# Expert passes of a fused transformer kernel: the low-rank product in five parts, the gate's second product two slots later, the output sums two slots apart, and a new end

## The chip, the cores and the metric

The kernel runs on one core of one Trainium2 chip. The metric is the device time of one execution in microseconds; before the change it is 2830.43 us, the median of three runs (2828.27, 2830.43 and 2831.24). All data are 32-bit floats.

## The reference

Four layers follow one another over 8 items of 512 x 512: a stencil on a grid, a transformer block (attention with 16 heads and a feed-forward part), one expert feed-forward block per item, and a low-rank "safety" layer. The change touches what follows the expert blocks:

```python
def expert(x, e):                      # Wi[e]: 512x2048, Wo[e]: 2048x512
    h = gelu(x @ Wi[e] + bi[e])
    r = h @ Wo[e] + bo[e] + x
    return layernorm(r) * gamma[e] + beta[e]

def safety(y, score):                  # y: 8 x 512 x 512, after the expert
    U_o, V_o = gram_schmidt(U), gram_schmidt(V)        # 512 x 32 each
    basis = U_o @ V_o.T
    h1 = relu(y.mean(axis=1) @ gate_w1.T + gate_b1)    # 128 per item
    strength = sigmoid(h1 @ gate_w2.T + gate_b2) * sigmoid(score)
    feats = (y @ basis) @ basis.T[:, :32]              # 512 x 32 per item
    return y + strength * (feats @ resp_w.T + resp_b + safety_bias)
```

`(y @ basis) @ basis.T[:, :32]` is one product of `y` with a 512 x 32 matrix. The kernel makes that matrix once and keeps it in the tile `wl3`.

## The kernel before, in words

The function `mlp_stage` runs 16 passes of the same form, q = 0 to 15: passes 0 to 7 are the feed-forward part of the transformer block, passes 8 to 15 the expert of items 0 to 7. A pass is `run(q, hooks)`. It has 56 slots. In slots 0 to 27 (four groups g of 7 slots, the seven products of a Strassen-like scheme) TensorE computes `u = A x B` from the weights `wi` and the turned input `bt`, VectorE (DVE) combines the seven products into `act`, and ScalarE (ACT) applies the gelu. In slots 28 to 55 (seven products of four slots, the name `y_28` to `y_52` giving the first slot) TensorE multiplies `act` with `wo`, and DVE adds the products into `x`. A slot is four 128x128x256 products, eight records in the trace. The products `u`, `y` and, in the last pass, a few small ones share six PSUM buffers (tag `u`); everything else that TensorE writes in this stage shares two (tag `tr`).

Everything else of a pass is hung onto the slots: `at(hooks, s, f)` calls f just before the products of slot s are issued. Each engine executes its own instructions strictly in the order in which they were written (`pin` keeps it), so a hook's instruction that has to wait holds back whatever stands behind it on its engine. DMA issues of the SyncE queue (SP) are ordered by the framework. All small products go through the helper `mm` (line 1137 of the profile), all transposes through `tp` (L1140), additions on DVE through `add` (L1143) and on GpSimd (POOL) through `gadd` (L1146).

The hooks that matter here:

- Passes 0 to 7 do the Gram-Schmidt steps of U and V (`gs_b`, the last of the 32 at slot 53 of pass 7). At slot 1 of pass 8 `low_rank` makes `wl3` from the result `qm`: it normalises `qm` (`square`, L1163; `inverse_norm`, a power on POOL at L1168; a scaling at L1201), turns it (`qtr`, copied to `qd`), and makes three small products, `pg`, `ph` and `pw`, each of which takes the DVE copy of the one before (`gram`, `hmat`). `wl3` is first read at slot 38 of pass 9.
- Passes 9 to 15 carry the tail of the item before, o = q - 1: `tail_norm` (slot 8, layer norm), `tail_turn` (slots 29 to 35, `ytr`, then `yT` on ACT, which also sums over the rows into `pool`), `tail_gamma` (37, DVE, L1569), `tail_feats` (38, product `pf`, copied to `ft`), `gate` (39, product `pg`, then two DVE instructions at L1617 and L1618 that make `h1`), `strength` (40, product `pz`, sigmoid on ACT, L1625), `add_beta` (42, DVE, then 128x2048 on POOL) and `tail_out` (50 to 53, one product `po` each, then on DVE at L1649 `x += st * po`; after each second one the rows go to DRAM).
- The same passes prepare the next one: `turn` (41, 43, 45, 47: `btr`), `w_quads` on POOL (46 and 50), `b_quads` on DVE (50: eight additions of 128x256, tiles `tb` and `bt`), and at slot 2 of the next pass `add_row`, 128x2048 on POOL.
- In pass 15 the first half of its own tail runs at slots 49 to 55 on rows 0 and 1. What follows the last slot works on rows 2 and 3: norm, turn, `pf`, gamma, beta, `gate` over the sum of both halves of `pool`, `strength`, and four times `tail_out`, where `po` is here the sum of two products (`rw` and `rb`).

Of the kernel before, what the change touches and what calls it, by code (L numbers as in the profile page):

```python
# [11 lines left out]
F32 = mybir.dt.float32  # L12
# [4 lines left out]
ALU = mybir.AluOpType  # L17
# [3 lines left out]
NB = 8  # L21
S = 512
D = 512
P = 128
R = 4
# [4 lines left out]
KC = D // P  # L30
RK = 32
# [1077 lines left out]
def mlp_stage(tc, a, small, xp, io, wo8, x1d, ident, eidx, sigs, layernorm, rstd_of, phalf, wl3, g2, b1, first):  # L1109
# [15 lines left out]
    nc = tc.nc  # L1125
# [3 lines left out]
    with ExitStack() as ctx:  # L1129
# [6 lines left out]
        def mm(out, lhsT, rhs, start, stop):  # L1136
            pin(nc.tensor.matmul(out, lhsT=lhsT, rhs=rhs, start=start, stop=stop))  # L1137

        def tp(out, src, idn=ident):
            pin(nc.tensor.transpose(out, src, idn))  # L1140

        def add(out, x, y, op=ALU.add):
            pin(nc.vector.tensor_tensor(out, x, y, op))  # L1143

        def gadd(out, x, y, op=ALU.add):
            pin(nc.gpsimd.tensor_tensor(out, x, y, op))  # L1146
# [13 lines left out]
        def square(src, other, tag):  # L1160
            junk = ap.tile([n, D], F32, name=f"junk_{tag}", tag="tmp", bufs=4)
            s = small.tile([n, 1], F32, name=f"{tag}_s", tag=f"{tag}_s")
            pin(nc.vector.tensor_tensor_reduce(junk, src, other, 1.0, 0.0, ALU.mult, ALU.add, s))  # L1163
            return s

        def inverse_norm(n2):
            d = small.tile([n, 1], F32, name="gs_d", tag="gs_d")
            pin(nc.gpsimd.tensor_tensor(d, n2, phalf[:n], ALU.pow))  # L1168
            pin(nc.vector.tensor_scalar(d, d, GS_EPS, None, ALU.add))
            r = small.tile([n, 1], F32, name="gs_r", tag="gs_r")  # L1170
            pin(nc.vector.reciprocal(r, d))
            return r
# [22 lines left out]
            if i + 1 < RK:  # L1195
                gs_a(i + 1)

        def low_rank():

            r = inverse_norm(square(qm, qm, "gn"))  # L1200
            pin(nc.vector.tensor_scalar(qm, qm, r, None, ALU.mult))  # L1201
            tr = ps.tile([P, KC, n], F32, name="qtr", tag="tr")
            for c in range(KC):
                tp(tr[:, c, :], qm[:, c * P : (c + 1) * P], ident[:n, :n])
            qd = ap.tile([P, KC, n], F32, name="qd", tag="beta", bufs=2)
            pin(nc.vector.tensor_copy(qd, tr))
            pg = ps.tile([RK, RK], F32, name="pg", tag="tr")
            for c in range(KC):
                mm(pg, qd[:, c, RK:n], qd[:, c, RK:n], c == 0, c == KC - 1)
            g = small.tile([RK, RK], F32, name="gram", tag="gram", bufs=1)  # L1210
            pin(nc.vector.tensor_copy(g, pg))
            ph = ps.tile([RK, RK], F32, name="ph", tag="tr")
            mm(ph, g, qm[0:RK, 0:RK], True, True)
            h = small.tile([RK, RK], F32, name="hmat", tag="hmat", bufs=1)
            pin(nc.vector.tensor_copy(h, ph))
            pw = ps.tile([P, KC, RK], F32, name="pw", tag="tr")
            for c in range(KC):
                mm(pw[:, c, :], qm[0:RK, c * P : (c + 1) * P], h, True, True)
            pin(nc.vector.tensor_copy(wl3, pw))


        b2 = ap.tile([P, D], F32, name="b2row", tag="bo_e", bufs=1)
# [333 lines left out]
        def tail_norm(q, rows):  # L1556

            if q not in outs:
                outs[q] = dict(
                    ft=ap.tile([P, P], F32, name=f"ft_{q}", tag="ft"), pooled=[],  # L1560
                )
            v = [xs[q][:, r, :] for r in rows]
            layernorm(v, v, LN_EPS2, "ln2", pin)
# [32 lines left out]
        def tail_feats(q, rows):  # L1596
            ys = outs[q]["ys"]
            pf = ps.tile([P, P], F32, name=f"pf_{q}_{rows[0]}", tag="tr")
            for c in range(KC):
                for i, r in enumerate(rows):  # L1600
                    mm(
                        pf[r * RK : (r + 1) * RK, :], wl3[:, c, :], ys[c][:, i, :],
                        c == 0, c == KC - 1,
                    )
            m = slice(rows[0] * RK, (rows[-1] + 1) * RK)
            pin(nc.vector.tensor_copy(outs[q]["ft"][m, :], pf[m, :]))
# [22 lines left out]
        def add_beta(q):  # L1629
# [2 lines left out]
            pin(nc.vector.scalar_tensor_tensor(beta, rb, st, beta, ALU.mult, ALU.add))  # L1632
            gadd(x, x, beta[:, None, :].to_broadcast([P, R, D]))

        def tail_out(q, rows):
            t = outs[q]
            x, ft, st = xs[q], t["ft"], t["st"]
            last = q == NQ - 1
            for r in rows:
                po = ps.tile(  # L1640
                    [P, D], F32, name=f"po_{q}_{r}", tag="u" if last else "tr",
                    bufs=6 if last else 2,
                )
                m = slice(r * RK, (r + 1) * RK)
                mm(po, ft[m, :], rw[m, :], True, not last)
                if last:
                    mm(po, ones[m, :], rb[m, :], False, True)
                pin(
                    nc.vector.scalar_tensor_tensor(x[:, r, :], po, st, x[:, r, :], ALU.mult, ALU.add)  # L1649
                )  # L1650
                if r % 2:
                    nc.sync.dma_start(
                        a["out"][q - NB].rearrange("(p r) f -> p r f", r=R)[:, r - 1 : r + 1, :],
                        x[:, r - 1 : r + 1, :],
                    )


        def at(hooks, s, f, *args):
            hooks.setdefault(s, []).append(lambda: f(*args))
# [8 lines left out]
        for q in range(NQ):  # L1668
            hooks = {}
            nx = q + 1 if q + 1 < NQ else None  # L1670

            at(hooks, 0, load_wo, q)
            if nx:
                if nx >= NB:
                    at(hooks, 45, load_extra, nx)
                at(hooks, 2, load_x, nx)
                for g in range(NG):
                    at(hooks, 7 * (g + 1), load_wi, nx, g)
            if 1 <= q <= NB:
                at(hooks, 4, lambda q=q: nc.sync.dma_start(x2d[q - 1], xs[q - 1]))  # L1680

            at(hooks, 2 if q else 26, add_row, q)
            at(hooks, 7, w_quads, q, 2, gadd)
            at(hooks, 14, w_quads, q, 3, gadd)
            for g in range(NG):
                at(hooks, 18 + 2 * g, t13, q, g)
            if nx:
                if nx < NB:
                    at(hooks, 33, norm, nx)
                for c in range(KC):  # L1690
                    at(hooks, 41 + 2 * c, turn, nx, c)
                at(hooks, 50, b_quads, nx)
                at(hooks, 46, w_quads, nx, 0, gadd)
                at(hooks, 50, w_quads, nx, 1, gadd)
            if q < NB:
                for i, s in enumerate((4, 18, 30, 53) if q else (18, 24, 30, 53)):
                    at(hooks, s, gs_b, 4 * q + i)
            if q == 0:
                at(hooks, 8, gs_a, 0)
                at(hooks, 10, load_constants)  # L1700
                at(hooks, 38, constants)
            if q == NB:
                at(hooks, 1, low_rank)
            elif q > NB:
                every = range(R)
                o = q - 1
                at(hooks, 8, tail_norm, o, every)
                for c in range(KC):
                    at(hooks, 29 + 2 * c, tail_turn, o, every, [c])
                at(hooks, 37, tail_gamma, o, every)  # L1710
                at(hooks, 38, tail_feats, o, every)
                at(hooks, 39, gate, o)
                at(hooks, 40, strength, o)
                at(hooks, 42, add_beta, o)
                for r in range(R):
                    at(hooks, 50 + r, tail_out, o, [r])
            if q == NQ - 1:
                half = range(0, 2)
                at(hooks, 49, tail_norm, q, half)
                for c in range(KC):  # L1720
                    at(hooks, 51 + c, tail_turn, q, half, [c])
                at(hooks, 55, tail_feats, q, half)
                at(hooks, 55, tail_gamma, q, half)
            run(q, hooks)
        q, half = NQ - 1, range(2, 4)
        x, beta = xs[q], extra[q][1][2]
        gadd(x[:, 0:2, :], x[:, 0:2, :], beta[:, None, :].to_broadcast([P, 2, D]))
        tail_norm(q, half)
        tail_turn(q, half, range(KC))
        tail_feats(q, half)  # L1730
        tail_gamma(q, half)
        add(x[:, 2:4, :], x[:, 2:4, :], beta[:, None, :].to_broadcast([P, 2, D]))
        gate(q)
        strength(q)
        tail_out(q, range(R))


# [86 lines left out]
```

## Time and profile before

The profile is of one execution of 2828.87 us; its span (first to last instruction) is 2826.4 us.

| what | value |
|---|---|
| median of three runs | 2830.43 us |
| profiled execution, its span | 2828.87 us, 2826.4 us |
| busy share of PE, DVE, ACT, POOL | 97%, 69%, 35%, 53% |
| mean granted TensorE clock | 0.989 |
| pass 7 (the last of the feed-forward part) | 98.45 us |
| pass 8 | 110.58 us |
| passes 9 to 14, each | 108.8 us |
| pass 15, slots 0 to 55 | 108.55 us |
| from the last product of slot 55 to the end of the span | 25.37 us |

PE is TensorE, PEld its weight loads, SPq the issue of DMAs. A pass is counted from the start of its first product `u` to that of the next pass, so its length says how far the pass is from the bare 98.45 us of the products. In lines of the timeline the first number is the start, the second the time from the first start to the last end of the group; `x8` is the number of records; a bracket names how long the engine sat idle before it and what ended the wait.

### The profile page before, as it was taken

The page shows a single profiled execution, that of the slowest core. Times are in us where ns is not written, and L with a number is a line of the kernel's source. Part 1 is how long each engine was busy: PE and PEld are TensorE (multiplying, and loading weights), DVE is VectorE, ACT ScalarE, POOL GpSimd, SP SyncE. Part 2 cuts the span into 40 slices and gives each one's busy share as a digit, 9 for nine tenths or more (in the row PEclk, how much of TensorE's full clock was granted, in tenths as well). Part 3 has the DMA queues.
Part 4 walks back from the last instruction along what each step waited for, and adds up shares of the span by engine and source line. Part 5 has one row for each costly group of instructions (what it writes and reads, how often), then busy time and mean ns, then how long its engine had stood idle before and what let it go on. Part 6 is the DMA issues. An engine that isn't in the chain of part 4 may idle for free.

```text
span 2826.4 us, 39775 instructions
## 1 busy us (share of the span) xinstructions
PE 2731.6 (97%) x14646; PEld 2013.2 (71%) x14646; DVE 1942.6 (69%) x3583; ACT 1003.3 (35%) x2133; POOL 1502.6 (53%) x1080
## 2 busy tenths in 40 slices
PE   5999999999999998999999999999999999999997
PEld 3455555555555554888888888887888888888885
DVE  6889898888888766576756666655466565556654
ACT  1466666666666666211211211111121121121120
POOL 3455555555555553566555656564455455445532
PEclk9999999999999999999999999999999999999998
DMA  9665757666665554642444253343224233133110
GB/s 303 220 211 173 235 176 239 203 210 215 190 228 187 162 156 144 190 125 71 120 140 123 51 157 123 80 122 123 98 68 138 78 105 124 63 131 112 45 71 30
DMA packets 190399, 405.60 MB, mean 144 GB/s; under 512 B 24104, under 2 KB 28784, under 8 KB 183934
## 3 DMA queue, kind: packets, MB, share of 16 engines
q1 hardware_dynamic: 185192, 391.93, 41.8%
q0 software_dynamic: 3680, 11.07, 3.1%
q8 instruction: 116, 1.90, 0.3%
q14 instruction: 77, 0.63, 0.1%
q10 hardware_dynamic: 1334, 0.07, 0.0%
HBM read 367.32 MB, written 31.50 MB: 141 GB/s over the span
## 4 chain that ended last, share of the span: by engine, by line
PE 81%; DVE 13%; ACT 2%; issue 1%; POOL 0%; DVEq 0%; POOLq 0%; ACTq 0%
PE u L1137 27%; PE y L1137 24%; PE tr L546 6%; PE s L543 4%; PE ctx L543 4%; PE o L543 3%; PE pv L543 3%; PE pq L543 3%; PE pk L543 2%; DVE bt L973 2%; DVE tb L1143 2%; DVE x L663 1%; DVE pt L998 1%; ACT bt L978 1%; DVE act L1143 1%
## 5 line engine op out<-in xcount | busy, mean ns | idle before, releaser
L1137 PE MATMUL y<-wo,act 128*128 128x256 f32 x2560 | 578.9, 381 | 0.0
L950 POOL TENSOR_TENSOR bt<-bt,mk 128x1024 f32<-128x1024 f32 x256 | 543.2, 2143 | 63.8 <-DMA bt<-in_bias 62.9
L1137 PEld LDWEIGHTS y<-wo,act 128*128 128x128 f32 x2560 | 479.3, 190 | 82.2 <-issue 20.5
L978 ACT ACTIVATE bt<-bt,mn 128x512 f32<-128x512 f32 x512 | 365.5, 715 | 116.3 <-DVE mn L973 116.2
L546 PEld LDWEIGHTS tr<-ident,bt 128*128 128x128 f32 x2048 | 228.1, 141 | 168.8 <-issue 115.5
L1137 PE MATMUL u<-bt,wi 128*128 128x256 f32 x1440 | 332.4, 381 | 0.0
L973 DVE CUSTOM_DVE_ANT_0 bt<-s,bt 128x512 f32<-128x512 f32 x512 | 330.4, 683 | 0.0
L1143 DVE TENSOR_TENSOR act<-u,u 128x512 f32<-128x512 f32 x256 | 173.4, 687 | 212.8 <-PE u L1137 138.0
L1137 PEld LDWEIGHTS u<-bt,wi 128*128 128x128 f32 x1440 | 274.6, 191 | 37.6
L546 PE MATMUL tr<-ident,bt 128*128 128x128 f32 x2048 | 280.0, 278 | 19.3 <-DVE pt L998 8.1
L998 DVE COPY pt<-tr 128x512 f32<-128x512 f32 x256 | 175.9, 687 | 110.6 <-PE tr L546 110.3
L1137 PE MATMUL u<-tb,ws 128*128 128x256 f32 x1024 | 242.3, 379 | 0.0
L1137 PE MATMUL y<-t,s 128*128 128x256 f32 x1024 | 234.1, 380 | 0.0
L1137 PEld LDWEIGHTS u<-tb,ws 128*128 128x128 f32 x1024 | 195.0, 190 | 26.7
L1000 ACT COPY pt<-tr 128x512 f32<-128x512 f32 x256 | 148.3, 579 | 180.1 <-PE tr L546 177.7
L1146 POOL TENSOR_TENSOR t<-wo,t 128x512 f32<-128x512 f32 x64 | 104.6, 1650 | 198.2 <-PE y L1137 198.2
L1137 PEld LDWEIGHTS y<-t,s 128*128 128x128 f32 x1024 | 190.6, 190 | 23.8
L1143 DVE TENSOR_TENSOR x<-y,x 128x512 f32<-128x512 f32 x96 | 64.6, 686 | 182.5 <-PE y L1137 128.5
L1449 ACT ACTIVATE act<-act,bi 128x512 f32<-128x512 f32 x128 | 83.9, 712 | 292.2 <-DVE act L1143 292.1
L1449 ACT ACTIVATE act<-act,b 128x512 f32<-128x512 f32 x128 | 82.9, 712 | 292.5 <-DVE act L1143 292.5
L543 PE MATMUL s<-kt,qt 32*128 32x512 f32 x1024 | 170.8, 643 | 2.1 <-DVE mn L973 1.1
L1143 DVE TENSOR_TENSOR u<-u,u 128x512 f32<-128x512 f32 x192 | 131.3, 684 | 59.5 <-PE u L1137 59.5
(313 smaller groups left out, 4282.4 us busy)
## 6 DMA issues: line engine op xcount, KB each, us to landing
bt<-in_bias SPq DMA_DIRECT2D x256, 512.0 KB
wo<-in_W SPq DMA_DIRECT2D x32, 1024.0 KB
wi<-in_Wi SPq DMA_DIRECT2D x32, 1024.0 KB
wo<-in_Wo_e SPq DMA_DIRECT2D x32, 1024.0 KB
wi<-in_W SPq DMA_DIRECT2D x28, 1024.0 KB
gq<-coef_q SPq DMA_DIRECT2D x21, 512.0 KB
x1d<-x SPq DMA_DIRECT2D x8, 1024.0 KB
x<-x1d SPq DMA_DIRECT2D x8, 1024.0 KB
```

Of the source, the lines that this page charges most:

```text
L543: pin(nc.tensor.matmul(out, lhsT=lhsT, rhs=rhs, start=start, stop=stop))
L546: pin(nc.tensor.transpose(out, src, ident))
L663: pin(nc.vector.tensor_tensor(out, x, y, op))
L950: nc.gpsimd.tensor_tensor(bt, bt, mask[b, r][:, None, :].to_broadcast([P, 2, S]), ALU.add)
L973: nc.vector.tensor_tensor_reduce(bt[:, i, :], ss[h], bt[:, i, :], -1.0, 3.0e38, ALU.add, ALU.min, mn)
L978: nc.scalar.activation(bt[:, i, :], bt[:, i, :], AF.Exp, bias=mn, scale=-1.0, accum_out=sums[b, c, r][:, h : h + 1],)
L998: pin(nc.vector.tensor_copy(pt[:, :, r % 2, :], tr))
L1000: pin(nc.scalar.copy(pt[:, :, r % 2, :], tr))
L1137: pin(nc.tensor.matmul(out, lhsT=lhsT, rhs=rhs, start=start, stop=stop))
L1143: pin(nc.vector.tensor_tensor(out, x, y, op))
L1146: pin(nc.gpsimd.tensor_tensor(out, x, y, op))
L1449: nc.scalar.activation(acts[g][:, k, :], acts[g][:, k, :], func, bias=bi[:, j : j + 1])
```

## The change

1. `low_rank` takes a part number. Part 0 (normalising) runs at slot 5 of pass 8, part 1 (`qtr`, `qd`) at 11, part 2 (`pg`, `gram`) at 14, part 3 (`ph`, `hmat`) at 16, part 4 (`pw`, `wl3`) at 20. Before, all ran at slot 1.
2. `strength` moves from slot 40 to slot 41 in passes 9 to 15, where it stands behind the transposes of `turn`.
3. `tail_out` is divided into `tail_sum` (the product) and `tail_add` (the addition and the DMA). In passes 9 to 14 the four rows move from slots 50, 51, 52, 53 to 49, 51, 53, 55. Pass 15 keeps 50 to 53.
4. The code behind the last slot is written out anew. `pg` is accumulated by TensorE from both halves of `pool`: four products with the first half ahead of the transposes, four with the second half between the four steps of `pf`. The addition of the two halves on DVE goes. Gamma stands before `ft`, beta moves to POOL, the four sums `po` stand before `strength`, and the four additions behind it.

```diff
-        def low_rank():
+        lr = {}
+
+        def low_rank(part):
-            r = inverse_norm(square(qm, qm, "gn"))
-            pin(nc.vector.tensor_scalar(qm, qm, r, None, ALU.mult))
+            if part == 0:
+                r = inverse_norm(square(qm, qm, "gn"))
+                pin(nc.vector.tensor_scalar(qm, qm, r, None, ALU.mult))
+            elif part == 1:
...
+            elif part == 2:
...
             if q == NB:
-                at(hooks, 1, low_rank)
+                for i, s in enumerate((5, 11, 14, 16, 20)):
+                    at(hooks, s, low_rank, i)
...
-                at(hooks, 40, strength, o)
+                at(hooks, 41, strength, o)
                 at(hooks, 42, add_beta, o)
                 for r in range(R):
-                    at(hooks, 50 + r, tail_out, o, [r])
+                    at(hooks, (50 + r) if q == NQ - 1 else (49 + 2 * r), tail_out, o, [r])
...
         tail_norm(q, half)
+        pg = ps.tile([P, 1], F32, name=f"pg_{q}", tag="u", bufs=6)
+        for c in range(KC):
+            mm(pg, gw1[:, c, :], t["pooled"][0][:, c : c + 1], c == 0, False)
         tail_turn(q, half, range(KC))
-        tail_feats(q, half)
         tail_gamma(q, half)
-        add(x[:, 2:4, :], x[:, 2:4, :], beta[:, None, :].to_broadcast([P, 2, D]))
-        gate(q)
-        strength(q)
-        tail_out(q, range(R))
+        pf = ps.tile([P, P], F32, name=f"pf_{q}_2", tag="u", bufs=6)
+        for c in range(KC):
+            for i, r in enumerate(half):
+                mm(
+                    pf[r * RK : (r + 1) * RK, :], wl3[:, c, :], t["ys"][c][:, i, :],
+                    c == 0, c == KC - 1,
+                )
+            mm(pg, gw1[:, c, :], t["pooled"][1][:, c : c + 1], False, c == KC - 1)
+        m = slice(half[0] * RK, (half[-1] + 1) * RK)
+        h1 = small.tile([P, 1], F32, name=f"h1_{q}", tag="h1")
+        pin(nc.vector.tensor_copy(t["ft"][m, :], pf[m, :]))
+        pin(nc.vector.tensor_scalar(h1, pg, 1.0 / S, gb1, ALU.mult, ALU.add))
+        pin(nc.vector.tensor_scalar(h1, h1, 0.0, None, ALU.max))
+        t["h1"] = h1
+        gadd(x[:, 2:4, :], x[:, 2:4, :], beta[:, None, :].to_broadcast([P, 2, D]))
+        for r in range(R):
+            tail_sum(q, r)
+        strength(q)
+        for r in range(R):
+            tail_add(q, r)
```

## The prediction

> **What bounds the kernel now.** I read first the chain that ended last, on the page. TensorE holds it:
>
> ```profile
> PE 81%; DVE 13%; ACT 2%; issue 1%; POOL 0%; DVEq 0%; POOLq 0%; ACTq 0%
> ```
>
> So I compared the passes next, in the table of stretches, cut where a pass's first product starts (columns: length, then busy time of PE, PEld, DVE, ACT, POOL, granted clock, DMA):
>
> ```profile
> 1830.82:1929.27 98.45, 98.45 (x466) 86.68 (x465) 52.65 (x99) 15.27 (x25) 55.91 (x43) 1.00 0.41 121
> 1929.27:2039.85 110.58, 104.32 (x488) 91.10 (x487) 50.79 (x72) 16.88 (x26) 54.60 (x35) 0.95 0.30 103
> 2148.64:2257.41 108.77, 107.83 (x531) 90.84 (x531) 63.95 (x86) 21.69 (x36) 56.94 (x35) 1.00 0.31 105
> 2801.03:2826.40 25.37, 10.57 (x51) 6.07 (x50) 9.57 (x19) 2.67 (x9) 2.73 (x2) 0.58 0.10 42
> ```
>
> Pass 7 is TensorE without a gap, 98.45 us. Pass 8 takes 110.58, 12.13 more. An expert pass with a tail takes 108.77, of which TensorE is idle for 0.94. Behind the last slot come 25.37 us in which it works 10.57. What the change can win lies in those three places. I read them in the timeline.
>
> **Part 1, the low-rank product in pass 8.** The timeline of its start, TensorE and DVE:
>
> ```profile
> 1929.11 1.89 PE L1137 MATMUL u<-bt,wi 128*128 128x256 f32 x8
> ...
> 1931.20 4.49 POOL L1146 TENSOR_TENSOR x<-x,bo_e 128x2048 f32<-128x2048 f32 x1
> ...
> 1931.63 4.33 DVE L1201 TENSOR_SCALAR qm<-qm,gs_r 64x512 f32<-64x512 f32 x1
> ...
> 1936.11 0.66 PE L1140 MATMUL qtr<-ident,qm 64*128 64x64 f32 x4 [5.11 <-DVE qm L1201]
> ...
> 1938.84 1.91 PE L1137 MATMUL pw<-hmat,qm 32*128 32x32 f32 x8 [0.27 <-DVE hmat L1215]
> ```
>
> TensorE stops at 1931.0 and is back at the pass's own products at 1940.75: 9.75 us. And it comes back slow. The table of stretches again:
>
> ```profile
> 1931.47:1934.88 3.41, 0.00 (x0) 0.00 (x0) 3.37 (x2) 1.48 (x2) 3.41 (x1) 1.00 1.05 399
> 1934.88:1938.29 3.41, 1.30 (x13) 1.04 (x14) 1.69 (x3) 0.00 (x0) 0.81 (x1) 0.50 1.07 407
> 1941.71:1945.12 3.41, 3.41 (x10) 2.69 (x9) 0.55 (x1) 0.00 (x0) 0.00 (x0) 0.50 0.83 295
> 1945.12:1948.53 3.41, 3.41 (x17) 3.02 (x16) 1.02 (x3) 0.00 (x0) 1.27 (x1) 1.00 0.03 12
> ```
>
> The clock is 0.50 from 1934.88 to 1945.12; of this 4.37 us are the pass's products, which lose half, 2.2. Together 11.9, which is the 12.13. This is what the Trainium skill says in "TensorE: Matmul & The Clock Gate" (Part 1): a window of about 3.4 us without work halves the clock, and a busy one restores it. By the row of the stall alone part 1 would be worth less than 9.75 us, with the gate less than 12.1.
>
> What stays is the small products' own time. Scaled to the full clock from the rows above: `qtr` 0.2, `pg` 0.25 (0.61 at half clock), `ph` 0.1, `pw` 0.95 (1.91 at half clock), 1.5 in all. Against the split speaks a rule of the skill, "TensorEngine Tiling (Array Packing)", Key Properties: changing the tiling mode drains TensorE. All four products use part of the array (64\*128, 128\*32, 32\*32, 32\*128), and split they go back to the full array each time: 8 changes, where there were 5. The nearest row has the price: a `po` (32\*128) between two slots of `y` costs 2.97 - 1.73 = 1.24 us (starts 2241.60 and 2244.57 below; 1.73 is a slot), and its two records of 512 columns should take 0.86 by the `y` records' 0.216 for 256; so 0.38 for a pair of changes. `pf` has 1.10 - 0.86 = 0.25. Four pairs at 0.3 are 1.2, bounds 1.0 and 1.6. The rest is 1.5 + 1.2 = 2.7, and the gain **12.13 - 2.7 = 9.4 us** (8.5 to 10.1; without the drains it would be 10.6).
>
> It holds only if no part waits. Part 0 is a chain over DVE, POOL and DVE: 0.7 for the square, about 0.6 for the power, 0.3, then L1201, which took 4.33 because the 128x2048 addition on POOL ran from 1931.20 to 1935.69 and the scaling ended just behind it. In the changed order that addition stands ahead of part 0's power on POOL and is done by about 1931; next come additions of 1.27 us, so L1201 should wait for one or two of them. From slot 5 (1929.27 + 8.65 = 1937.9) it is done by 1943, and `qtr` stands at slot 11, 1948.3: 5 us of cover. DVE's additions behind it (slots 5 and 6) and the gelu after them come up to 4 us late; TensorE needs their PSUM buffer six slots later (10.4 us). The other parts have two to four slots (3.5 to 6.9 us) for one DVE copy of 0.2 to 0.4. `wl3` is read a pass later. If the cover for part 1 were gone for 4 us or more, the clock would fall again.
>
> **Part 2, the gate's second product.** An expert pass, timeline of TensorE, and of DVE for the `tb` line:
>
> ```profile
> 2219.59 1.97 PE L1137 MATMUL y<-wo,act 128*128 128x256 f32 x8
> 2222.18 0.35 PE L1137 MATMUL pz<-h,gw 128*128 128x1 f32 x2 [0.62 <-DVE h L1618]
> ...
> 2241.60 1.12 PE L1137 MATMUL po<-rw,ft 32*128 32x512 f32 x2
> ...
> 2244.57 1.12 PE L1137 MATMUL po<-rw,ft 32*128 32x512 f32 x2
> ...
> 2247.94 1.12 PE L1137 MATMUL po<-rw,ft 32*128 32x512 f32 x2 [0.32 <-DVE x L1649]
> ```
>
> ```profile
> 2240.47 4.55 DVE L1143 TENSOR_TENSOR tb<-bt,tb 128x256 f32<-128x256 f32 x1
> ```
>
> `pz` could start at 2219.59 + 1.73 = 2221.32 and 0.1 for the hand-over; it starts 0.76 later, waiting for `h1`. One slot on, behind `btr` (0.43), it stands at about 2223.5; `h1` is ready at 2222.03, 1.5 us of cover (1.0 in pass 15, which has no `btr`). Gain 7 x 0.75 = **5.2 us** (0.62 to 0.8 each: 4.3 to 5.6). The sigmoid, DVE's two instructions and POOL's 128x2048 addition come about 0.8 us later by the clock. Behind that on POOL stand `w_quads` and the next `add_row`, first needed in the next pass; behind it on SP the load of the next beta row. Nothing near waits.
>
> **Part 3, the output sums.** The third `po` comes 3.37 after the second, where 2.97 is the rule: 0.40 lost, since it needs the buffer of the first, whose DVE addition stands behind `b_quads`, and one `tb` there took 4.55 for its usual 0.4 (POOL's `add_row` again). In the new order the first `po` is added ahead of `b_quads`, so the third finds its buffer. The fourth (slot 55, about 2253.4) needs the addition of the second, which now stands behind `b_quads`: `add_row` from about 2240.9 to 2245.5, eight `tb` and `bt` until 2248.6, the addition until 2249.4. 4.0 us of cover. Gain 6 x 0.4 = **2.4 us** (0 to 2.6), as many products and changes as before. (0.76 + 0.40 is more than the 0.94 idle, because a record counts as busy until its modelled end.) The second output DMA is issued about 2.5 us later, behind the loads of `wo_0` and `wo_1` and ahead of `wo_2` and `wo_3`, which wait for slot 55 anyway; POOL first reads `wo` some 25 us after.
>
> **Part 4, the end.** Timeline:
>
> ```profile
> 2808.36 1.92 PE L1137 MATMUL pf<-yT,wl 128*32 128x128 f32 x16 [0.26 <-ACT yT L1589]
> ...
> 2813.36 1.84 PE L1137 MATMUL pg<-pool,gw 128*128 128x1 f32 x8 [3.08 <-DVE pool L1143]
> ...
> 2820.09 2.73 DVE L1649 SCALAR_TENSOR_TENSOR x<-po,st,x 128x512 f32<-128x512 f32 x4 [3.25 <-PE po L1137]
> ```
>
> Removed from the path: 3.05 us between `pf` and `pg` (`ft`, gamma, beta, the sum of the halves). Added: `pf` and the second half of `pg` alternate, 1.92 + 1.84 and up to eight changes of mode at half clock. A pair, 0.25 to 0.38 at full clock, is bounded by 0.25 and 0.8 here; I take 0.5, near twice the nearest row's: 2.0. So they end at 2808.36 + 3.76 + 2.0 = 2814.1. Then the four `po` (2816.28 to 2820.09, 3.8), then `pz` and its sigmoid behind them, where they ran beside: 0.56 + 0.4 + 0.25. With 0.2 for the change, 2819.3 against 2820.09: 0.8 gained at half clock (-0.5 to 2). Should the clock hold, everything there shrinks: 2808.2, + 1.75 + 4 x 0.3, + 0.2 + 1.95 + 0.35 + 0.7 = 2814.3, gain 5.8. The first half of `pg` (about 0.95 us) shortens the empty stretch after the last slot from 4.19 to 3.2, shorter than one window; but sparse ones count too, and what follows is transposes that wait for ACT. Mostly the clock will fall somewhere on the way: **2.0 us** (-0.5 to 5.8).
>
> **The sum.** 9.4 + 5.2 + 2.4 + 2.0 = 19.0. The span of 2826.4 becomes 2807.4, the profiled execution 2828.87 becomes 2809.9. What lies around the span (2.47) is not touched, and the median, 1.56 above the profiled execution, becomes 2830.43 - 19.0 = **2811.4 us**, 0.67% less.
>
> **The rivals.**
> - The clock holds to the end (part 4 at 5.8): 2807.6. For it speaks the gap of 3.2; against it that a window with only 1.04 us of work was enough to halve the clock elsewhere in this trace.
> - Part 1 moves its wait: L1201 stays behind POOL's additions for 5 us or more, and `qtr` waits at slot 11 for 2 to 6 us, with the clock falling. Part 1 then brings 3 to 6: 2815 to 2818. For it speaks the row of 4.33; against it the cover of 5 us and that the additions there are short, so that DVE got between two of them in 1.50 elsewhere (the `tb` ahead of the one shown).
> - Slower: the fourth `po` waits for DVE. Its addition ahead stands behind `b_quads`, and each of those eight needs SBUF while POOL adds. If they end more than 4.0 us late, each us costs 6; from 4.0 + 19.0/6 = 7.2 us on the kernel is slower, at 9 us by 11 (2841). Against it: only one `tb` in eight waited for POOL before, and POOL has nothing after `add_row`.
> - It does nothing that can be measured: only if part 1 failed whole and the others halved, about 2826.
>
> **How the numbers follow.** Forecast 66% (2808.5 to 2815), clock holds 15%, part 1 half 13%, nothing 3%, slower 3%. The range 2806 to 2818 holds the first three: its low end is the sum of the good ends (10.1 + 5.6 + 2.6 + 5.8 = 24.1), its high end part 1 halved with the low ends of part 2 and half of the rest (4.5 + 4.3 + 2.4 + 1 = 12.2). A change of 0.2% (5.7 us) is about what a measurement of this kernel can tell from none: faster 0.94, same 0.03, slower 0.03.
>
> **What would show it.** Pass 8 at about 101.2 us with a clock of 1.00 throughout and no wait at `qtr`; passes 9 to 14 at 107.6; no wait at `pz` for L1618 and none at the third `po`; about 24 us behind the last slot. Wrong would be: a row of `qtr` or `po` with a wait above 1 us, a pass 8 above 104, or an end longer than 25.4.

## The result, and the profile after

The changed kernel takes 2808.33 us (median of four runs, 2807.21 to 2809.32) against 2829.93 us before (2828.27 to 2831.24): a ratio of 0.9925, with a 95% interval of 0.9911 to 0.9939. The profiled execution took 2809.32 us, its span 2807.5. Of all executions named in this document one, of the kernel with the undivided low-rank product at slot 5, ran slowly at a granted clock of 0.751 (3551.64 us); it counts in the median given there, but not in the ratio.

In the chain that ended last TensorE's share has grown from 81% to 86%, and DVE's has shrunk from 13% to 9%: DVE's pieces in the expert passes are gone.

```profile
PE 86%; DVE 9%; ACT 2%; DMA 2%; issue 1%; SPq 0%; DVEq 0%; ACTq 0%; POOL 0%
```

The same stretches of the changed kernel: passes 7 and 8, an expert pass, and what lies behind the last slot (columns as before: length, busy time of PE, PEld, DVE, ACT and POOL, granted clock, DMA):

```profile
1832.73:1931.18 98.45, 98.45 (x466) 86.68 (x465) 54.25 (x98) 15.27 (x25) 59.07 (x44) 1.00 0.42 121
1931.18:2032.36 101.18, 101.18 (x488) 88.10 (x487) 49.21 (x74) 16.88 (x26) 51.35 (x35) 1.00 0.33 112
2139.88:2247.41 107.53, 107.53 (x532) 90.94 (x531) 64.21 (x86) 21.67 (x36) 56.90 (x35) 1.00 0.31 106
2785.23:2807.50 22.27, 11.42 (x57) 6.09 (x57) 8.28 (x17) 2.66 (x9) 5.06 (x3) 0.69 0.12 48
```

In passes 8 to 15 TensorE's busy time now equals the length: no wait is left. By passes, from the two profiles:

| stretch | before | after | difference | predicted |
|---|---|---|---|---|
| pass 8 | 110.58 | 101.18 | -9.40 | -9.4 |
| passes 9 to 14, together | 652.6 | 645.15 | -7.5 | -6.9 (6 x 0.75 + 2.4) |
| pass 15 | 108.55 | 107.72 | -0.83 | -0.75 |
| behind the last slot | 25.37 | 22.27 | -3.1 | -2.0 |
| sum | | | -20.8 | -19.0 |

The spans differ by 18.9 only, because pass 1 of the feed-forward part starts 1.91 us later in the profile of after (1241.87 against 1239.96), in code that the change does not touch. The profiles of the twelve runs below put that start between 1239.9 and 1243.2, so this is scatter of the first half, and it goes into every run's time. The lengths of the passes carry none of it, and the experiments are read by them: where an edit does not touch it, a pass repeats within 0.04 us. Only pass 8 with the undivided product at slot 1 varies more, from 110.5 to 111.1.

Pass 8, timeline of the changed kernel:

```profile
1927.95 4.50 POOL L1146 TENSOR_TENSOR x<-x,bo_e 128x2048 f32<-128x2048 f32 x1
...
1942.76 1.11 DVE L1204 TENSOR_SCALAR qm<-qm,gs_r 64x512 f32<-64x512 f32 x1
...
1950.11 0.46 PE L1140 MATMUL qtr<-ident,qm 64*128 64x64 f32 x4
...
1955.87 0.44 PE L1137 MATMUL pg<-qd 128*32 128x32 f32 x8
...
1959.89 0.24 PE L1137 MATMUL ph<-qm,gram 32*32 32x32 f32 x2
...
1967.17 1.07 PE L1137 MATMUL pw<-hmat,qm 32*128 32x32 f32 x8
```

None has a bracket: TensorE came to each and found its input there. The scaling (L1204, L1201 before) takes 1.11 us, since POOL's long addition is over 10 us earlier; it ends 6.2 us ahead of `qtr`.

An expert pass, TensorE, then ACT and POOL, then DVE:

```profile
2214.81 0.28 PE L1137 MATMUL pz<-h,gw 128*128 128x1 f32 x2
...
2230.26 1.12 PE L1137 MATMUL po<-rw,ft 32*128 32x512 f32 x2
...
2234.96 1.12 PE L1137 MATMUL po<-rw,ft 32*128 32x512 f32 x2
...
2239.66 1.12 PE L1137 MATMUL po<-rw,ft 32*128 32x512 f32 x2
...
2244.36 1.12 PE L1137 MATMUL po<-rw,ft 32*128 32x512 f32 x2
```

```profile
2215.01 0.58 ACT L1370 COPY bt<-btr 128x512 f32<-128x512 f32 x1 [12.03 <-PE btr L1140]
2215.61 1.28 ACT L1633 ACT_TABLE_LOAD   x1
2216.91 0.26 ACT L1633 ACTIVATE st<-pz,gb 128x1 f32<-128x1 f32 x1
...
2218.23 4.53 POOL L1146 TENSOR_TENSOR x<-x,beta 128x2048 f32<-128x2048 f32 x1 [4.00 <-DVE beta L1640]
```

```profile
2233.64 4.55 DVE L1143 TENSOR_TENSOR tb<-bt,tb 128x256 f32<-128x256 f32 x1
...
2240.31 0.74 DVE L1656 SCALAR_TENSOR_TENSOR x<-po,st,x 128x512 f32<-128x512 f32 x1
```

`pz` and the third `po` wait no more, four even steps of 4.70 us. The 4.55 us of one `tb` are still there, but the addition behind it that frees a buffer for the fourth `po`, that of the second (done at 2241.05), ends 3.3 us ahead of it. One thing was not foreseen: ACT now loads the sigmoid's table (1.28 us) between the copy of `btr` and the sigmoid. Before, it stood in front of an idle ACT, long before `pz`:

```profile
2211.75 1.28 ACT L1625 ACT_TABLE_LOAD   x1
```

So POOL's addition starts 78.35 us into the pass, where it was 76.41 (2225.05 - 2148.64): 1.94 later, not 0.8.

The end, TensorE, and DVE for the last line:

```profile
2789.39 1.03 PE L1140 MATMUL ytr<-ident,x 128*128 128x128 f32 x4 [3.40 <-DVE x L85]
...
2792.06 0.64 PE L1137 MATMUL pf<-yT,wl 128*32 128x128 f32 x4
...
2792.63 0.59 PE L1137 MATMUL pg<-pool,gw 128*128 128x1 f32 x2
...
2793.15 0.64 PE L1137 MATMUL pf<-yT,wl 128*32 128x128 f32 x4
...
2796.41 2.11 PE L1137 MATMUL po<-rw,ft 32*128 32x512 f32 x8
...
2800.16 0.44 PE L1137 MATMUL pz<-h,gw 128*128 128x1 f32 x2
...
2801.19 2.73 DVE L1656 SCALAR_TENSOR_TENSOR x<-po,st,x 128x512 f32<-128x512 f32 x4
```

A step of `pf` and `pg` takes 1.09 us (2793.15 - 2792.06), and the four together 4.35 (2796.41 - 2792.06). The granted clock is 0.50 from 2790.06 to 2800.30, then 1.00 for 3.41 us, then 0.50 again.

### The profile page after: what moved, and what is told of

Same layout as the page of the kernel before. It is cut to its first block, busy times and chain, and to the rows that moved or that the text cites. A ratio compares the mean times of both kernels' runs of the same rounds, so it can differ in the third digit from the quotient of the medians.

```text
span 2807.5 us, 39790 instructions
## 1 busy us (share of the span) xinstructions
PE 2729.1 (97%) x14654; PEld 2011.6 (72%) x14654; DVE 1942.0 (69%) x3581; ACT 1002.8 (36%) x2133; POOL 1503.9 (54%) x1081
## 4 chain that ended last, share of the span: by engine, by line
PE 86%; DVE 9%; ACT 2%; DMA 2%; issue 1%; SPq 0%; DVEq 0%; ACTq 0%; POOL 0%
PE y L1137 28%; PE u L1137 28%; PE tr L546 6%; PE s L543 4%; PE ctx L543 4%; PE o L543 3%; PE pv L543 3%; PE pq L543 3%; PE pk L543 2%; DVE bt L973 2%; DVE x L663 2%; DVE pt L998 1%; DMA Wo<-in_Wo 1%; ACT bt L978 1%; PE po L1137 1%; PE btr L1140 1%
```

## The experiments

Ratios are against the kernel before on the same chip, with a 95% interval. Passes are from each run's profile, cut as above; the length of pass 8 is that of passes 7 and 8 less 98.45.

**Each part alone, on the kernel before.** Part 1:

```diff
-                at(hooks, 1, low_rank)
+                for i, s in enumerate((5, 11, 14, 16, 20)):
+                    at(hooks, s, low_rank, i)
```

> Part 1 alone. My theory (wait of 9.75 us plus 2.2 us lost at half clock, less 2.7 us of small products with their changes of mode): pass 8 about 101.2 us instead of 110.58, clock 1.00 throughout, passes 9 to 15 unchanged (108.8, 108.55), in all -9.4 us, near 2820.5. Rival (the split only moves the wait, TensorE waits at qtr for the scaling): pass 8 at 104 to 108 and the clock at 0.50 once more, -3 to -6 us.

Measured: 2819.94 us, 0.9966 (0.9952 to 0.998); pass 8 101.17 us, the other passes unchanged. The rival is out: nothing waits at `qtr`.

Part 2:

```diff
-                at(hooks, 40, strength, o)
+                at(hooks, 41, strength, o)
```

> Part 2 alone. Theory A, the parts add up: passes 9 to 14 at 108.0 us, pass 15 at 107.8, in all -5.2 us. Theory B, a wait moves: POOL's addition of beta comes 0.8 us later, so add_row and the eight additions of b_quads end later while TensorE is 0.75 us earlier; the third po then waits 1 to 1.7 us instead of 0.4, passes 9 to 14 stay at 108.5 to 109.3 us, only pass 15 gains 0.8, in all between -2.5 and +2.5 us. I hold B for likelier.

Measured: **2846.22 us, 1.0053 (1.0037 to 1.007), 16 us slower**. Theory B has the place of the wait right, the third `po`, and the size wrong: it expected at most 2.5 us more. Timeline of the third expert pass, and two passes and three of the 3.41 us stretches of the clock in the table of stretches:

```profile
2233.33 4.53 POOL L1146 TENSOR_TENSOR x<-x,beta 128x2048 f32<-128x2048 f32 x1 [4.00 <-DVE beta L1632]
...
2248.75 4.68 POOL L1146 TENSOR_TENSOR x<-x,bo_e 128x2048 f32<-128x2048 f32 x1
2248.99 5.06 DVE L1143 TENSOR_TENSOR bt<-bt,bt 128x256 f32<-128x256 f32 x2
...
2255.44 1.12 PE L1137 MATMUL po<-rw,ft 32*128 32x512 f32 x2 [2.33 <-DVE x L1649]
```

```profile
2041.87:2154.99 113.12, 110.80 (x531) 92.42 (x531) 66.22 (x86) 20.39 (x35) 57.34 (x35) 0.97 0.28 92
2154.99:2264.91 109.92, 107.59 (x531) 90.92 (x531) 66.23 (x86) 21.68 (x36) 57.33 (x35) 1.00 0.31 103
...
2138.77:2142.18 3.41, 1.22 (x6) 0.74 (x4) 3.41 (x6) 0.00 (x0) 1.53 (x1) 1.00 0.00 0
2142.18:2145.59 3.41, 3.29 (x5) 1.60 (x6) 3.28 (x6) 0.00 (x0) 0.00 (x0) 0.50 0.38 154
2251.41:2254.82 3.41, 1.70 (x8) 1.14 (x7) 3.41 (x5) 0.00 (x0) 2.02 (x1) 1.00 0.00 0
```

Every one of the six passes has the wait of 2.3 us at the third `po`. In two of them that is all (109.9 us); in four the clock falls to 0.50 behind it, for two stretches or one, and they take 113.1 to 113.2 or 111.6. So part 2 alone removes the wait of `pz`, 0.76 us a pass, but lets the wait at the third `po` grow from 0.40 to 2.3, and behind four of the six the clock adds 1.6 or 3.3 us.

Part 3:

```diff
-                    at(hooks, 50 + r, tail_out, o, [r])
+                    at(hooks, (50 + r) if q == NQ - 1 else (49 + 2 * r), tail_out, o, [r])
```

> Part 3 alone. My theory: no wait at the third po, the wait of pz for h1 stays at 0.6 us; passes 9 to 14 at 108.4 us, pass 15 unchanged, in all -2.4 us. Rival (the wait goes from the third to the fourth po, whose buffer is free only behind b_quads): 108.8, nothing.

Measured: 2827.19 us, 0.9993 (0.9986 to 1.0); passes 9 to 14 108.37 us, which is 0.40 less each, 2.4 in all. As expected; the wait did not go to the fourth `po`. The time of the runs alone would not have settled it.

Part 4, the whole new end as in the diff of the change:

```diff
-        tail_feats(q, half)
         tail_gamma(q, half)
-        add(x[:, 2:4, :], x[:, 2:4, :], beta[:, None, :].to_broadcast([P, 2, D]))
-        gate(q)
-        strength(q)
-        tail_out(q, range(R))
...
+        for r in range(R):
+            tail_sum(q, r)
+        strength(q)
+        for r in range(R):
+            tail_add(q, r)
```

> Part 4 alone. By the trace of the changed kernel a pair of pf and pg costs 1.09 us at half clock, so the stretch behind the last slot takes 22.3 us instead of 25.4: -3.1 us if the clock falls where it fell there. Rival (the clock's windows lie otherwise against the end and it holds for longer): 18 to 21 us behind the last slot. All passes as before.

Measured: 2826.46 us, 0.9988 (0.9982 to 0.9995); 22.3 us behind the last slot, passes 9 to 15 as before. As expected, the rival is out. The old end takes 25.0 to 25.6 us in the eight profiles that have it, the new one 22.3 to 22.5 in three.

By passes the four alone are -9.4, +17.5 (passes 9 to 15), -2.4 and -3.1, in all +2.6; the change has -20.8. The parts are not independent: it is part 2 that needs another.

**Parts 2 and 3 together** (both lines above):

> Parts 2 and 3 together. Theory: part 3 takes away the wait that part 2 alone makes (six waits of 2.3 us at the third po with the clock falling behind them), so passes 9 to 14 at 107.5 us as in the changed kernel, pass 15 at 107.7, in all -8.3 us, although the two alone gave +16 and -2.4. Rival (other parts of the change were needed too): passes above 108.

Measured: 2822.3 us, 0.9973 (0.9964 to 0.9982); passes 9 to 14 107.52 us, no wait at `po`. Part 3 takes the whole loss of part 2 away, and nothing else of the change is needed for it.

**What delays the third `po`.** Part 2 alone, with POOL's long addition moved out of the way of `b_quads` in passes 8 to 15:

```diff
-            at(hooks, 2 if q else 26, add_row, q)
+            at(hooks, 10 if q > NB - 1 else 2 if q else 26, add_row, q)
-                at(hooks, 40, strength, o)
+                at(hooks, 41, strength, o)
```

> Part 2 alone, and in passes 8 to 15 add_row at slot 10 in place of slot 2, so that POOL does not add 128x2048 while b_quads runs. If POOL's hold on DVE makes the third po wait: no wait of po above 0.1 us, the clock at 1.00, passes 9 to 14 at 107.5 to 107.7 us, where part 2 alone had 109.9 to 113.2. In pass 8 the scaling L1201 takes about 1.1 us instead of 4.33, so the wait at qtr is about 2 us and pass 8 at 103 to 107. In all -12 to -16 us. Rival (the wait comes from the place of the po additions behind b_quads, whatever POOL does): po still waits 1 us or more, passes 109 to 111.

Measured: 2848.39 us, 1.0068 (1.0051 to 1.0085). The wait at `po` is gone in all six passes, so POOL's addition was its cause. Pass 8 takes 104.9 us; the scaling there took 0.48 and `qtr` waited 1.25. But passes 9 to 14 take 111.8 to 112.3. The forecast of the time missed, since the addition now holds up something else:

```profile
2165.87 4.52 POOL L1146 TENSOR_TENSOR x<-x,bo_e 128x2048 f32<-128x2048 f32 x1
2165.93 8.95 DVE L85 TENSOR_SCALAR x<-x,ln_mv,ln_r 128x512 f32<-128x512 f32 x4 [1.13 <-POOL ln_r L71]
...
2175.54 5.41 PE L1137 MATMUL u<-bt,wi 128*128 128x256 f32 x16 [2.78 <-DVE act L1143]
```

The four scalings of `tail_norm`, 0.5 us each elsewhere, take 8.95 together beside POOL's additions, the combining of the products behind them is late, and TensorE waits 2.78 us for a PSUM buffer. DVE beside a long addition of POOL is the cause again, in another place. In four of the six passes the clock falls for 3.41 us behind this wait, in the other two a second wait of 0.9 follows.

**What the table load costs.** Part 2 alone, `strength` ahead of `turn` in slot 41:

```diff
-                at(hooks, 40, strength, o)
+                if q > NB:
+                    at(hooks, 41, strength, q - 1)     # ahead of the turn hooks
```

> Part 2 alone, but strength stands ahead of turn in slot 41, so that ACT loads the table of the sigmoid while it waits, and not between the copy of btr and the sigmoid (1.28 us). Theory: POOL's addition of beta comes 1.3 to 1.7 us earlier than in part 2 alone, the third po waits 0.7 to 1.3 us instead of 2.3, the clock stays at 1.00, passes 9 to 14 at 108.6 to 109.2 us, in all -1.5 to +2 us against the +16 of part 2 alone. Rival (the table load is hidden anyway): as part 2 alone, waits of 2.3 us, +10 us or more.

Measured: 2827.97 us, 0.9996 (0.9987 to 1.0005); passes 9 to 14 108.5 us, a little under the forecast; the third `po` waits 0.97. The table is loaded 11.7 us before the sigmoid (2214.09 and 2225.79), and POOL's addition starts 76.4 us into the pass, as in the kernel before. So the delay of 1.94 us comes from `strength` standing behind `turn` on ACT and on TensorE, not from the slot. By the two ratios that is some 16 us between two orders of the same instructions in one slot.

**The division or the place.** The undivided low-rank product at slot 5:

```diff
-                at(hooks, 1, low_rank)
+                at(hooks, 5, low_rank)
```

> The kernel before with the undivided low-rank product at slot 5 in place of slot 1: tells whether the later place or the division brings part 1. POOL's 128x2048 addition is over by then, so the scaling (L1201) should take about 1.1 us and not 4.33. My theory (TensorE waits for the chain over DVE and POOL wherever it stands undivided): TensorE still idles about 4 us ahead of qtr, the clock falls to 0.50 again, pass 8 at 107.5 to 110, -1 to -3 us. Rival (the place was the fault, POOL's addition above all): pass 8 at 103 to 105, -6 us or better.

Measured: 2828.68 us, 0.9997 (0.9988 to 1.0006); pass 8 109.6 us. The scaling takes 1.11 us there, and still `qtr` waits 4.1 and the clock falls. The reason stands on DVE: the squaring has to follow the two additions of the slot before, and starts at 1940.32, when TensorE's last product has ended (1939.07). So the later place alone brings 1.0 us. The rival has something in it, though: in the run with `add_row` at slot 10 the product stood undivided at slot 1, and pass 8 took 104.9 us. Keeping POOL's addition away was worth 5.7 us there, if at a cost in the passes behind it. The whole 9.4, with no wait left, came only with the division.

**Versions of the end.** The changed kernel once more, as the measure:

> The changed kernel itself, as the measure for the two that follow: ratio 0.9925, the stretch behind the last slot 22.3 us, give or take the place of the clock's windows.

Measured: 2809.0 us, 0.9927 (0.9911 to 0.9944), 22.46 us behind the last slot. Then with the products of `rb` moved ahead:

```diff
+        for r in range(R):
+            po = t["po", r] = ps.tile([P, D], F32, name=f"po_{q}_{r}", tag="u", bufs=6)
+            m = slice(r * RK, (r + 1) * RK)
+            mm(po, ones[m, :], rb[m, :], True, False)
         tail_turn(q, half, range(KC))
```

> The changed kernel with the four products of rb (ones) ahead of the transposes, behind the first half of pg, where TensorE is idle: they take about 1 us there at full clock and 1.95 us less behind pf. The empty stretch shrinks to about 2.2 us. Theory: the stretch behind the last slot 20.3 us (-2.0 against the changed kernel), and 16 to 18 if the clock then holds at 1.00. Rival (the sums were hidden behind the gate's path): under 0.7 us.

Measured: 2807.98 us, 0.9918 (0.9901 to 0.9934); 20.72 us behind the last slot, 1.7 less. The products take 1.14 us in a stretch that was empty. The clock fell nevertheless and stayed at 0.50 to the end. And with `pg` ahead of `pf` in each step and `strength` ahead of the sums:

> As the last, with pg ahead of pf in each of the four steps, and strength ahead of the four sums. Theory: pz and the sigmoid run while ft is copied and po is made, 0.6 to 1.1 us less than the last: the stretch behind the last slot 19.2 to 19.7 us at half clock. Rival (po then waits for pz as long as pz waited for po): no difference to the last.

Measured: 2807.11 us, 0.992 (0.9904 to 0.9937); 19.96 us, another 0.76 less. By the times of the runs neither is clear of the changed kernel; the stretch shows both.

**A version that beats both.** On top of it, the `po` products of passes 9 to 14 in pairs, two at slot 49 and two at 53:

```diff
+        def tail_pair(q, rows):
+            for r in rows:
+                tail_sum(q, r)
+            for r in rows:
+                tail_add(q, r)
...
-                    at(hooks, (50 + r) if q == NQ - 1 else (49 + 2 * r), tail_out, o, [r])
+                    if q == NQ - 1:
+                        at(hooks, 50 + r, tail_out, o, [r])
+                    elif r % 2 == 0:
+                        at(hooks, 49 + 2 * r, tail_pair, o, [r, r + 1])
```

> The last but with the po products of passes 9 to 14 in pairs, two at slot 49 and two at slot 53, both products ahead of both additions. A pair uses two different quarters of TensorE's rows; at the end of the kernel four such groups ran together in the time of one. Theory: a pair costs one pair of mode changes and about the time of one product (1.25 to 1.6 us), so the passes take 105.0 to 105.8 us instead of 107.5, in all -10 to -15 us against the version before it, near 2794. Rival (each product is bound by the drain and not by the array, or the buffers make it wait): passes at 106.7 or more, under -5 us.

Measured: **2791.45 us, 0.9863 (0.9847 to 0.988)**; passes 9 to 14 105.04 us, 2.48 less than in the changed kernel, which is two times the 1.24 us of one `po`. A pair, four records where one product has two:

```profile
2233.94 1.13 PE L1137 MATMUL po<-rw,ft 32*128 32x512 f32 x4
```

1.13 us, where one product took 1.12: the second of a pair costs nothing.

## Why the prediction was right, point by point

- **Part 1** was right in its size and in its working: 9.4 us predicted, 9.40 measured, by itself and in the whole. The small products with their changes of mode took 101.18 - 98.45 = 2.73 us (2.7). The cover at `qtr` was 6.2 us (5). The later place alone is not enough (1.0 us, the run with one piece at slot 5). But 5.7 of the 9.4 came without the division when POOL's addition was moved; the prediction read the row of 4.33 rightly and did not ask for that.
- **Parts 2 and 3** came to 8.3 us together (7.6). But the bookkeeping, 5.2 for the one and 2.4 for the other, was wrong: part 2 by itself costs 16 us. The step that failed is "DVE's two instructions and POOL's 128x2048 addition come about 0.8 us later ... Nothing near waits". It left out the table load, so the delay was 1.94, and it looked for the waiters of the moved step without asking who waits for POOL's *next* addition: `b_quads`, and through it the third `po`. In the change as a whole that wait cannot arise, because part 3 takes the first `po` ahead of `b_quads`. The forecast was right there because part 3 was worked out with the later POOL, and its cover of 4.0 us (3.3 measured) swallowed the error.
- **Part 4** had the right mechanism, and its number was a middle between two cases. The clock fell, at 2790.06, 4.8 us behind the last slot and ahead of `pf`. For that case the working had a gain of 0.8 us; measured to the same place, the first of the four last additions, it is 3.1: 2801.19 - 2785.23 = 15.96 us against 2820.09 - 2801.03 = 19.06. That 2.0 came closer was luck: it leaned on the held clock, which did not come. The mis-sized term is "a pair ... I take 0.5, near twice the nearest row's". One record of `pg`, or two of `pf` side by side, follow each other every 0.213 us at half clock, so the products of a step take 0.85 of its 1.09, and a pair of changes takes about 0.23. Over four steps that is 1.1 us. Another 0.5 was put at nothing: `pf` starts 6.83 us behind the last slot where it started at 7.33, since it no longer waits 0.26 for `yT`, and the first transposes still start at full clock (1.03 us for 1.27). The remaining 0.8 is spread over smaller terms: the products' own time (0.35), the way from the last `po` to the addition, and the 0.2 set aside for the change.
- The range held; the median, 2808.33, is 3.1 us below the forecast and just outside the 2808.5 to 2815 meant for it. It lies beside the 2807.6 of the rival with the held clock, but not for that rival's reason. Of the 3.1 us, 1.8 are the stretches (20.8 against 19.0). The rest is scatter: the median before came out 0.5 lower with a fourth run, and the medians differ by 21.6 us where the stretches differ by 20.8.
- The rival in which the change ends slower had its place nearly right: DVE held by POOL during `b_quads` until a `po` is late. The run with part 2 alone is that rival, at the third `po` instead of the fourth. In the change itself the fourth `po` still had 3.3 us of cover.

Left open: what makes the first half scatter by 3.4 us. None of the runs looked at it.

## What to carry to other kernels

A step that is moved by one slot also moves everything that its instructions release, queue by queue, to the next long instruction on each engine; follow it there before a gain is booked, and test the parts of a change alone, since one may pay for another. On an in-order engine the order within a slot can matter more than the slot: a table load or a copy that lands in front of a waited-for instruction is paid in full. Where TensorE has small products on a quarter of its rows, issue those on different quarters next to each other.

## What the runs showed of the hardware that was not expected

- In one execution the clock fell only at instants that lie whole windows of 3.413 us apart. In the run with part 2 alone it fell at 1937.38, 2142.18, 2367.45, 2480.09, 2701.96 and 2824.84 us, by the granted clock in quarter-microsecond stretches: distances of 60, 66, 33, 65 and 36 times 3.413 us. In all fourteen profiles every stretch at one clock, except the last, is whole windows long. The Trainium skill says so ("TensorE: Matmul & The Clock Gate", Part 1: the window runs freely). What the runs add: a window need not be empty. Those ahead of the four falls in the expert passes had 1.22, 2.09, 1.53 and 1.93 us of TensorE's work; with 1.70 and 1.90 in the other two passes it held, so the busy time of the records alone doesn't decide. So the same wait of 2.3 us cost 2.3, 3.9 or 5.6 us. That its place among the windows decides is what these instants suggest; no run shifted one wait against them.
- Two products on different quarters of the rows cost 1.13 us together where one costs 1.12, even between full-array products; with the change of mode paid once, a pair saves 1.24 us.
- A change of mode did not get dearer at half clock: about 0.23 us for a pair between `pf` and full-array products, against 0.25 at full clock for the same shapes.
